# Fewer identity products, later small products and two-block tiles in the first pass of a graph kernel

## The chip, the cores and the metric

The kernel runs on one core of one Trainium2 chip. The metric is the device time in microseconds (us), the median of several runs. A profile of one execution goes with it; its span runs from the first to the last instruction and is about one microsecond shorter than the time. Engine names in the profile: PE is TensorE (products), PEld its weight loads, DVE is VectorE, ACT is ScalarE, POOL is GpSimd, SP is the engine that issues most loads.

## The reference, cut to what matters

Two graph layers on x (3327 nodes, 512 features) with one adjacency matrix (3327 x 3327, sparse in content, stored dense, all float32).

```python
h = relu(layernorm(x))
h1 = relu(adj @ (h @ W1) + b1)            # W1: 512 x 128
x = x + adj @ (h1 @ W2) + b2              # W2: 128 x 512
h = relu(layernorm(x))
# attention over the nonzero entries of adj, and a second aggregate adj @ h, both gated
e = where(adj != 0, exp(-leaky_relu(s_left[:, None] + s_right[None, :], 0.01)), 0)
x_a = (e / (sum(e) + 1e-5)) @ (h @ W_sa)
x_b = adj @ (h @ W_gcnb) + b_gcnb
x = x + sigmoid(attn_a * x_a + attn_b * x_b)
```

## The kernel before

The rows are padded to 26 blocks of 128, and the columns of the transposed adjacency are cut into six chunks of 512 and one of 256 (chunks 0 to 6). The kernel goes through the adjacency twice. The first pass makes adj @ (h @ W1) and at the same time finds, for every block of 32 columns, which rows hold a nonzero, so that the second layer can gather those rows alone. The second pass makes adj @ h1, then @ W2, and the second layer's features. A third part combines the gathered rows.

At its head, while the first blocks of x are loaded, TensorE multiplies an identity with itself:

```python
WAKE = 30
...
    awake = bank(psB, "awake")
    for _ in range(WAKE):
        nc.tensor.matmul(awake[:, :P], ident, ident, start=True, stop=True)
```

Loads of the adjacency go through a pool of eight buffers of 128 x 512. The helper can put n blocks into one buffer; the first pass asks for one block at a time, the second pass for as many as fit (two in the chunk of 256 columns):

```python
        def load_adj(j, c, name, n=1):
            c0, w = chunks[c]
            n = min(n, NB - j)
            t = adjp.tile([P, CW], F32, tag="adj", name=f"{name}_{c}_{j}")
            t = t[:, : n * w].rearrange("p (k i) -> p k i", i=w)
            rows = adjT[j * P : (j + n) * P, c0 : c0 + w]
            nc.sync.dma_start(t, rows.rearrange("(k p) i -> p k i", p=P))
            return t
```

The first pass, cut. Per block j and chunk c there is one big product into acc_u on TensorE and one row-maximum (`most`) on VectorE. In chunk 0 the blocks of x are normalized, transposed (pt), and multiplied by W1 (pu) on the way:

```python
        for c in range(NCH):
            c0, w = chunks[c]
            acc = bank(psA, f"acc_u_{c}")
            most = l0w.tile([P, MG, NB], F32, tag="most", name=f"most_{c}")
            for j in range(NB):
                if c == 0:
                    ...                       # load_x, normalize, turn_h (pt), make_u (pu)
                with queued(x_loaded[min(j + 4, NB - 1)] if c == 0 else None):
                    a = load_adj(j, c, "a1")[:, 0, :]
                added = nc.tensor.matmul(
                    acc[:, :w], u[j], a[:, :w], start=(j == 0), stop=(j == NB - 1)
                )
                with queued(scaled[min(j + 3, NB - 1)] if c == 0 else None):
                    nc.vector.tensor_reduce(
                        most[:, : w // GW, j], a[:, :w].rearrange("p (b i) -> p b i", i=GW),
                        axis=AX.X, op=ALU.max, apply_absolute_value=True,
                    )
                if j >= 2:
                    next(lists, None)         # one step of the previous chunk's lists
                if j % 3:
                    gather_behind(added)      # one gather of listed rows, on GpSimd
                ...
            chunk_end = make_g(c, acc)        # relu, transpose (pg), copies to g
            with tc.issue_after(chunk_end.ins):
                if c == 1:
                    load_weights()            # W2, the bias row b2 (b_row in the profile), W_sa, ...
                ...
            lists = make_lists(c, most)
            next(lists)
```

`load_weights` also has VectorE add 0.5 to the bias row, once it has landed. `make_lists` is a generator; each `yield` lets the loop above go one tile on. From the row-maxima it makes flags, a running count, offsets by two small products (p_off) and a shift by another (p_sh). Then, for one batch of column groups after another, VectorE makes comparisons (`at`), TensorE multiplies them with `step` in many small products (p_list), and VectorE turns the results into lists of rows (past, jb, row_h, row_a):

```python
            nc.vector.tensor_tensor(after[...], count[...], upto[...], ALU.subtract)
            p_off = bank(psB, f"p_off_{c}")
            nc.tensor.matmul(p_off[:, :n], before, count[:, :n], start=True, stop=True)
            nc.tensor.matmul(p_off[:, MG : MG + n], every, count[:, :n], start=True, stop=True)
            ...                                # offset, size, p_sh, step
            yield
            ...                                # column groups into batches of up to 18 rows of places
            for batch in batches:
                ...
                for i, q in batch:
                    r, k = rooms[i], col[i, q]
                    for h in range(2):
                        b = NQ * i + 2 * h + q - g0
                        nc.vector.tensor_scalar(                      # `at`
                            at[:, k : k + r, h, :],
                            place_row[:, : r * HALF].rearrange("p (k m) -> p k m", m=HALF),
                            offset[:, b : b + 1], None, op0=ALU.is_ge,
                        )
                    if (i, q) != batch[-1]:
                        yield
                pl = bank(psB, f"p_list_{f0}")
                for i, q in batch:
                    for k in range(col[i, q], col[i, q] + rooms[i]):
                        for h in range(2):
                            nc.tensor.matmul(                         # p_list
                                plv[h * HALF : (h + 1) * HALF, k, :], at[:, k, h, :],
                                step[:, NQ * i + 2 * h + q - g0, :], start=True, stop=True,
                            )
                yield
                ...                            # past, jb, row_h, row_a
                listed.update(batch)
                yield
```

A scheduler orders each engine's instructions after this program, so their places on an engine need not be those of the program text. After the first pass the vectors of weights for the scores are made: VectorE forms products of W_sa with a row (junk) and TensorE turns the columns (pw).

Of the kernel before, what the change touches and what calls it, by code (L numbers as in the profile page):

```python
# [19 lines left out]
CW = 512  # L20
# [4 lines left out]
LEAD = 3, 4  # L25
EH = 8
SEG = 4
WAKE = 30
LN_EPS = 1e-5
SUM_EPS = 1e-5  # L30
SLOPE = 0.01
# [15 lines left out]
def kernel(  # L47
# [20 lines left out]
    NB = NP // P  # L68
# [14 lines left out]
    def bank(pool, name):  # L83
        return pool.tile([P, CW], F32, tag="bank", name=name)
# [94 lines left out]
    def queued(*insts):  # L179

        behind = ExitStack()
        for inst in insts:
            if inst is not None:
                behind.enter_context(tc.issue_after(inst.ins))
        return behind
# [30 lines left out]
    with (  # L216
# [48 lines left out]
        x_loaded, scaled, h_turned, u_made = {}, {}, {}, {}  # L265
# [118 lines left out]
        def make_lists(c, most):  # L384


            c0, w = chunks[c]
            g0, n = c0 // GW, w // GW

            def small(shape, name, dtype, bufs=2):  # L390
                return l0w.tile(shape, dtype, tag=name, name=f"{name}_{c}", bufs=bufs)

            flag = small([P, MG, NB], "flag", BF16)
            nc.vector.tensor_scalar(flag[:, :n, :], most[:, :n, :], 0.0, None, op0=ALU.is_gt)

            upto = small([P, MG, NB], "upto", BF16)
            flat = "p b j -> p (b j)"
            nc.vector.tensor_tensor_scan(
                upto[:, :n, :].rearrange(flat), begin[:, :n, :].rearrange(flat),
                flag[:, :n, :].rearrange(flat), 0.0, op0=ALU.mult, op1=ALU.add,  # L400
            )
            count = small([P, MG], "count", BF16)
            nc.vector.tensor_copy(count[:, :n], upto[:, :n, NB - 1])
            after = small([P, MG, NB], "after", BF16)
            nc.vector.tensor_tensor(
                after[:, :n, :], count[:, :n].unsqueeze(2).to_broadcast([P, n, NB]),
                upto[:, :n, :], ALU.subtract,
            )
            p_off = bank(psB, f"p_off_{c}")
            nc.tensor.matmul(p_off[:, :n], before, count[:, :n], start=True, stop=True)  # L410
            nc.tensor.matmul(p_off[:, MG : MG + n], every, count[:, :n], start=True, stop=True)
            offset = small([P, MG], "offset", F32)
            nc.vector.tensor_copy(offset[:, :n], p_off[:, :n])
            nc.vector.tensor_tensor(
                size[:, g0 : g0 + n], p_off[:, MG : MG + n], limit[:, g0 : g0 + n], ALU.is_gt
            )


            step = steps[c % 2]
            p_sh = bank(psB, f"p_sh_{c}")  # L420
            nc.tensor.matmul(
                p_sh[:, : n * NB], shift, after[:, :n, :].rearrange(flat), start=True, stop=True
            )
            nc.vector.tensor_tensor(
                step[:, :n, :NB], p_sh[:, : n * NB].rearrange("p (b j) -> p b j", j=NB),
                upto[:, :n, :], ALU.add,
            )
            yield
            batches = []
            for i in range(c0 // P, (c0 + w) // P):  # L430
                for q in range(2 if rooms[i] else 0):
                    if not batches or sum(rooms[k] for k, _ in batches[-1]) + rooms[i] > CW // NT:
                        batches.append([])
                    batches[-1].append((i, q))
            for batch in batches:
                col = {}
                m = 0
                for i, q in batch:
                    col[i, q] = m
                    m += rooms[i]  # L440
                f0 = first[batch[0][0]] + batch[0][1] * rooms[batch[0][0]]
                at = l0w.tile([P, CW // NT, 2, HALF], BF16, tag="at", name=f"at_{f0}")
# [4 lines that stand above are left out]
                        nc.vector.tensor_scalar(  # L447
                            at[:, k : k + r, h, :],
                            place_row[:, : r * HALF].rearrange("p (k m) -> p k m", m=HALF),
                            offset[:, b : b + 1], None, op0=ALU.is_ge,  # L450
                        )
                    if (i, q) != batch[-1]:
                        yield
                pl = bank(psB, f"p_list_{f0}")
                plv = pl[:, : m * NT].rearrange("p (c j) -> p c j", j=NT)
                for i, q in batch:
                    for k in range(col[i, q], col[i, q] + rooms[i]):
                        for h in range(2):
                            nc.tensor.matmul(  # L459
# [4 lines that stand above are left out]
                past = l0w.tile([P, CW // NT, NB], BF16, tag="past", name=f"past_{f0}", bufs=1)  # L464
                nc.vector.tensor_tensor(
                    past[:, :m, :], plv[:, :, :NB],
                    place_col[:, f0 : f0 + m].unsqueeze(2).to_broadcast([P, m, NB]), ALU.is_le,
                )
                jb = l0w.tile([P, CW // NT], F32, tag="jb", name=f"jb_{f0}")
                nc.vector.tensor_reduce(jb[:, :m], past[:, :m, :], axis=AX.X, op=ALU.add)  # L470
                nc.vector.scalar_tensor_tensor(
                    jb[:, :m], jb[:, :m], float(P), plv[:, :, NB], op0=ALU.mult, op1=ALU.add
                )

                nc.vector.tensor_scalar(
                    row_h[:, f0 : f0 + m], jb[:, :m], float(NP - 1), None, op0=ALU.min
                )
                nc.vector.scalar_tensor_tensor(
                    row_a[:, f0 : f0 + m], jb[:, :m], float(NG), group_col[:, f0 : f0 + m],
                    op0=ALU.mult, op1=ALU.add,  # L480
                )
                listed.update(batch)
                yield
# [11 lines left out]
        for c in range(NCH):  # L495
            c0, w = chunks[c]
            acc = bank(psA, f"acc_u_{c}")
            most = l0w.tile([P, MG, NB], F32, tag="most", name=f"most_{c}")
            for j in range(NB):
                if c == 0:  # L500
                    if j + 4 < NB:
                        load_x(j + 4)
                    if j + 3 < NB:
                        normalize(j + 3)
                    if j + 2 < NB:
                        turn_h(j + 2)
                    if j + 1 < NB:
                        make_u(j + 1)
                with queued(x_loaded[min(j + 4, NB - 1)] if c == 0 else None):
                    a = load_adj(j, c, "a1")[:, 0, :]  # L510
                added = nc.tensor.matmul(  # L511
                    acc[:, :w], u[j], a[:, :w], start=(j == 0), stop=(j == NB - 1)
                )
# [6 lines that stand above are left out]
                    next(lists, None)  # L520
                if j % 3:
                    gather_behind(added)
                if c == 0 and j % 2 == 0:
                    with queued(scaled[min(j + 3, NB - 1)]):
                        next(constants, None)
            for work in (lists, constants):
                for _ in work:
                    pass
            chunk_end = make_g(c, acc)
            with tc.issue_after(chunk_end.ins):  # L530
                if c == 1:
                    load_weights()
                if 0 < c <= HUB_LOADS:
                    load_hub(c - 1)
            lists = make_lists(c, most)
            next(lists)

# [120 lines left out]
        for c in range(NCH):  # L658
            c0, w = chunks[c]
            acc = bank(psA, f"acc_g_{c}")  # L660
            per = CW // w
# [435 lines left out]
```

## Time and profile before

| | |
|---|---|
| time, median of 3 runs | 781.73 us (780.81 to 782.48) |
| span of the profile | 780.7 us |
| first pass, chunk 0 from its first big product | 13.50 to 67.36 us |
| first pass, chunks 1 to 6 | 67.36 to 224.86 us |
| second pass and the rest | 224.86 to 780.7 us |
| TensorE busy over the span | 755.4 us (97%) |
| VectorE busy over the span | 517.5 us (66%) |
| big products acc_u | 364 records, 580 ns each |
| row-maxima `most` | 182, 640 ns each |
| small products p_list | 456 records of 128 x 27, 186 ns each |

Each float32 product shows as two records, and records of neighbouring products overlap, so a record's length is not what it costs; the distance from start to start is. A line of a timeline has start, duration, engine, source line, operation, output and inputs, shapes and how many instructions it merges; square brackets name the idle time before it and what ended it. A line of waits has engine, what waited, for whom, then the total in us, how many times, and the longest.

### The profile page before, as it was taken

To read this page: it belongs to the slowest core of one execution; us is meant where nothing else is said; L and a number is where in the kernel's file an instruction comes from. 1 tells how busy PE (TensorE), PEld (TensorE's weight loads), DVE (VectorE), ACT (ScalarE), POOL (GpSimd) and SP (SyncE) were. 2 spreads that over 40 slices of the span, in tenths; PEclk is the share of its full clock that TensorE was granted. 3 is DMA by queue.
4 is the path that set the end of the run, shared out by engine and by line. 5 is a ranking of instruction groups with operands and counts; after the bars stand their busy time and mean duration, and the time that the engine had idled before them with its cause. 6 is when DMAs were issued, how large, how long until landed. Compare 5 with 4: busy or idle time off the path is not lost.

```text
span 780.7 us, 12235 instructions
## 1 busy us (share of the span) xinstructions
PE 755.4 (97%) x3647; PEld 415.5 (53%) x3647; DVE 517.5 (66%) x1658; ACT 185.5 (24%) x396; POOL 489.8 (63%) x513
## 2 busy tenths in 40 slices
PE   9999989999999999999999999999999999999995
PEld 8775434444544344344446456665665666655453
DVE  6768979999992876759577575555465464644542
ACT  6882000000000331403215212221221221311211
POOL 1400746666777777777773277677777777777720
PEclk9999999999999999999999999999999999999998
DMA  7888899889889999899998578688888888888840
GB/s 241 247 261 262 272 296 289 263 270 293 230 262 288 319 333 336 283 323 318 311 336 266 171 226 242 202 245 255 252 238 253 251 234 260 225 258 229 228 154 32
DMA packets 107099, 200.15 MB, mean 256 GB/s; under 512 B 17009, under 2 KB 30864, under 8 KB 107024
## 3 DMA queue, kind: packets, MB, share of 16 engines
q1 hardware_dynamic: 72800, 124.40, 48.7%
q0 software_dynamic: 25536, 63.74, 29.8%
q10 hardware_dynamic: 8688, 11.15, 4.3%
q8 instruction: 31, 0.51, 0.3%
q14 instruction: 44, 0.36, 0.2%
HBM read 179.39 MB, written 20.55 MB: 256 GB/s over the span
## 4 chain that ended last, share of the span: by engine, by line
PE 82%; DMA 7%; DVE 7%; issue 1%; ACT 1%; POOL 0%; SPq 0%; POOLq 0%; ACTq 0%; DVEq 0%
PE acc_u L511 16%; PE acc_g L665 14%; PE acc L809 13%; PE p_b L863 12%; PE p_a L870 11%; DMA a<-in_adjT_dram 6%; PE ptt L823 3%; PE pu L293 3%; PE acc_hub L624 2%; PE px L580 2%; PE p_list L459 2%; PE pt L285 1%; DVE junk L559 1%; DVE xb L583 1%; PE awake L100 1%
## 5 line engine op out<-in xcount | busy, mean ns | idle before, releaser
L139 POOL DMA_INDIRECT ae<-in_adjT_dram,row_a x228 | 244.2, 1071 | 145.2 <-DVE most L515 49.1
L139 POOL DMA_INDIRECT hr<-h_rows,row_h x140 | 143.5, 1025 | 47.0 <-issue 27.4
L511 PE MATMUL acc_u<-a,rows 128*128 128x512 f32 (+1 forms) x364 | 164.0, 580 | 1.5 <-DMA a<-in_adjT_dram 1.5
L665 PE MATMUL acc_g<-a,g 128*128 128x512 f32 (+1 forms) x364 | 156.4, 570 | 3.6 <-DMA a<-in_adjT_dram 3.4
L139 POOL DMA_INDIRECT rows<-h_rows,row_h x88 | 90.0, 1022 | 50.7 <-DVE e_hub L206 24.2
L515 DVE TENSOR_REDUCE most<-a 128x16 f32<-128x512 f32 (+1 forms) x182 | 111.1, 640 | 7.2 <-DMA a<-in_adjT_dram 6.8
L665 PEld LDWEIGHTS acc_g<-a,g 128*128 128x128 f32 x364 | 68.2, 192 | 80.1 <-issue 62.7
L863 PE MATMUL p_b<-W_g_sb,tyT 128*128 128x257 f32 x416 | 97.1, 386 | 0.8 <-ACT tyT L836 0.5
L870 PE MATMUL p_a<-W_sa_sb,tyT 128*128 128x512 f32 (+2 forms) x216 | 93.5, 577 | 0.0
L863 PEld LDWEIGHTS p_b<-W_g_sb,tyT 128*128 128x128 f32 x416 | 76.6, 189 | 30.8 <-DVE ae L206 7.3
L511 PEld LDWEIGHTS acc_u<-a,rows 128*128 128x128 f32 x364 | 63.9, 192 | 52.3 <-issue 45.8
L838 DVE COPY tyT<-ptt 128x512 f32<-128x512 f32 x51 | 34.9, 686 | 73.6 <-PE ptt L823 73.5
L809 PE MATMUL acc<-hr,ae 64*64 64x512 f32 x560 | 68.0, 607 | 0.0
L870 PEld LDWEIGHTS p_a<-W_sa_sb,tyT 128*128 128x128 f32 x216 | 41.0, 190 | 37.7 <-issue 35.9
L728 ACT ACTIVATE f<-f 128x2 f32<-128x2 f32 x26 | 5.3, 203 | 173.2 <-DVE f L727 145.8
L809 PE MATMUL acc<-rows,ae 64*64 64x512 f32 x352 | 42.5, 594 | 2.5 <-issue 1.8
L809 PEld LDWEIGHTS acc<-hr,ae 64*64 64x64 f32 x560 | 29.8, 136 | 23.4 <-issue 22.9
L302 ACT ACTIVATE gT<-acc_u,b_col 128x512 f32<-128x512 f32 (+1 forms) x7 | 4.6, 656 | 154.8 <-PE acc_u L511 97.9
L696 DVE TENSOR_TENSOR xb<-xb,b_row 128x512 f32<-128x512 f32 x26 | 17.7, 690 | 29.7 <-DMA xb<-in_x_dram 24.1
L559 DVE SCALAR_TENSOR_TENSOR junk<-rows,w_rows 128x512 bf16<-128x512 f32 x52 | 35.7, 687 | 1.9 <-ACT rows L201 0.9
L583 DVE TENSOR_TENSOR xb<-px,xb 128x512 f32<-128x512 f32 x26 | 16.9, 683 | 24.9 <-PE px L580 24.9
L823 PEld LDWEIGHTS ptt<-ident,ty 128*128 128x128 f32 x208 | 24.2, 141 | 14.2 <-issue 12.9
(142 smaller groups left out, 909.9 us busy)
## 6 DMA issues: line engine op xcount, KB each, us to landing
a<-in_adjT_dram SPq DMA_DIRECT2D x325, 256.0 KB, 4.0
h_rows<-rows SPq DMA_DIRECT2D x26, 260.0 KB, 4.1
x<-in_x_dram SPq DMA_DIRECT2D x26, 256.0 KB, 3.4
xb<-in_x_dram SPq DMA_DIRECT2D x26, 256.0 KB, 5.0
x<-xb ACTq DMA_DIRECT2D x26, 256.0 KB, 2.1
x1b<-x SPq DMA_DIRECT2D x26, 256.0 KB, 4.9
out_dram<-va SPq DMA_DIRECT2D x25, 256.0 KB
ae<-in_adjT_dram,row_a POOLq DMA_INDIRECT x228, 4.4
```

The costliest lines, as they stand in the source:

```text
L139: return nc.gpsimd.indirect_dma_start(out=dst, out_offset=None, in_=table, in_offset=bass.IndirectOffsetOnAxis(ap=rows, axis=0), bounds_ch ...
L293: nc.tensor.matmul(pu[:, :HID], hT[:, k, :], W1_sb[:, k, :], start=(k == 0), stop=(k == KD - 1))
L511: added = nc.tensor.matmul(acc[:, :w], u[j], a[:, :w], start=(j == 0), stop=(j == NB - 1))
L515: nc.vector.tensor_reduce(most[:, : w // GW, j], a[:, :w].rearrange("p (b i) -> p b i", i=GW), axis=AX.X, op=ALU.max, apply_absolute_value ...
L559: return nc.vector.scalar_tensor_tensor(junk, h, 1.0, w_rows[:, s, :], op0=ALU.mult, op1=ALU.mult, accum_out=into)
L583: nc.vector.tensor_tensor(x1, px, x1, ALU.add)
L665: added = nc.tensor.matmul(acc[:, :w], g[j], a[:, j % per, :], start=(j == 0), stop=(j == NB - 1))
L809: added = nc.tensor.matmul(taken[i]["acc"][h][q * HALF : (q + 1) * HALF, :], both[half_p, q * n + k, :], taken[i][k0][k][half_p, q, :D], s ...
L823: moved = nc.tensor.transpose(pt[:, k * P : (k + 1) * P], ty[h][:, k * P : (k + 1) * P], ident)
L838: last = nc.vector.tensor_copy(dst, src)
L863: nc.tensor.matmul(p_b[n][:, :WH], tyT[:, k, 0, :], W_g_sb[:, k, n * WH : (n + 1) * WH], start=(k == 0), stop=(k == KD - 1),)
L870: last = nc.tensor.matmul(p_a[:, c0:c1], tyT[:, k, 1, :], W_sa_sb[:, k, c0:c1], start=(k == 0), stop=(k == KD - 1),)
```

## The change

The change has three parts, all in the first pass. The head has 18 identity products instead of 30, to let TensorE go on to the first real work sooner. The generator of the lists yields once more before the products p_off, and after the last comparison of each batch too, so that a tile of other work lies between comparisons and the products that read them. And in the chunk of 256 columns, two blocks share one buffer and one load, as the second pass already has it. No arithmetic is added or removed but the twelve identity products.

```diff
-WAKE = 30
+WAKE = 18
@@ make_lists
                 upto[:, :n, :], ALU.subtract,
             )
+            yield
             p_off = bank(psB, f"p_off_{c}")
@@ make_lists, in each batch
                             offset[:, b : b + 1], None, op0=ALU.is_ge,
                         )
-                    if (i, q) != batch[-1]:
-                        yield
+                    yield
                 pl = bank(psB, f"p_list_{f0}")
@@ first pass
             acc = bank(psA, f"acc_u_{c}")
+            per = CW // w
             most = l0w.tile([P, MG, NB], F32, tag="most", name=f"most_{c}")
@@ first pass, for each j
-                with queued(x_loaded[min(j + 4, NB - 1)] if c == 0 else None):
-                    a = load_adj(j, c, "a1")[:, 0, :]
+                if j % per == 0:
+                    with queued(x_loaded[min(j + 4, NB - 1)] if c == 0 else None):
+                        tile_a = load_adj(j, c, "a1", per)
+                a = tile_a[:, j % per, :]
```

## The prediction

> **What bounds the kernel now.** I read the page first, then the windows of the first pass cut at each chunk's first product, then the waits of TensorE there, then the timeline of the two stretches that looked odd. The change touches only the first pass (0 to 225 us of the 780.7 us span), so only that pass is worked out.
>
> The windows give one row for each of chunks 2 to 6 (columns: length, busy time and instructions of each engine, granted clock, DMA share, GB/s):
>
> ```profile
> 93.84:126.31 32.47, 28.89 (x149) 12.88 (x147) 26.75 (x69) 0.69 (x1) 17.79 (x19) 0.95 0.91 293
> 126.31:154.28 27.97, 27.62 (x136) 11.64 (x135) 27.04 (x70) 0.69 (x1) 17.26 (x18) 1.00 0.88 269
> 154.28:180.07 25.79, 25.79 (x125) 11.40 (x124) 24.68 (x64) 0.69 (x1) 17.02 (x18) 1.00 0.91 281
> 180.07:205.89 25.82, 25.82 (x121) 11.29 (x119) 24.56 (x64) 0.69 (x1) 17.04 (x18) 1.00 0.89 270
> 205.89:224.86 18.97, 17.44 (x108) 10.50 (x107) 17.63 (x65) 0.69 (x1) 14.32 (x15) 1.00 0.74 207
> ```
>
> The reader should see two engines close together: TensorE (first busy column) is never idle in chunks 4 and 5, but VectorE (third) is busy for all but 1.1 to 1.3 us of them, and chunk 3 has 27.04 us of VectorE work in 27.97 us. Chunk 2 stands out with 32.47 us and a clock of 0.95. Chunk 6 has a low DMA share, 0.74. The waits of TensorE from 68 to 225 us:
>
> ```profile
> PE p_list L459 <- DVE at L447: 2.8, 2, 2.5
> PE acc_u L511 <- DMA a<-in_adjT_dram: 1.5, 5, 0.4
> PE p_sh L421 <- DVE after L405: 0.9, 1, 0.9
> PE p_off L410 <- DVE count L403: 0.2, 1, 0.2
> ```
>
> Only 5.4 us of real waiting, most of it in chunk 2. Its timeline shows why:
>
> ```profile
> 99.14 0.31 DVE L447 TENSOR_SCALAR at<-place_row,offset 128x384 bf16<-128x384 f16 x1
> 102.39 0.43 DVE L257 TENSOR_SCALAR b_row<-b_row 128x512 f32<-128x512 f32 x1 [2.94 <-DMA b_row<-in_b_dram]
> 102.73 1.23 DVE L447 TENSOR_SCALAR at<-place_row,offset 128x384 bf16<-128x384 f16 x5
> ...
> 100.35 0.20 PE L459 MATMUL p_list<-step,at 128*64 128x27 bf16 x1
> 103.10 1.42 PE L459 MATMUL p_list<-step,at 128*64 128x27 bf16 x35 [2.54 <-DVE at L447]
> ```
>
> The bias row's load lands late, VectorE stands behind it for 2.94 us, the comparisons `at` come late, and TensorE stands at the small product. The granted clock is then 0.78 from 101 to 106 us and 0.84 from 106 to 110. The head:
>
> ```profile
> 1.43 8.59 PE L100 MATMUL awake<-ident 128*128 128x128 f32 x60 [1.43 <-POOL ident masks.py:199]
> 6.22 1.50 ACT L201 ACTIVATE h<-x,ln_a 128x512 f32<-128x512 f32 x2
> 9.86 1.04 PE L285 MATMUL pt<-ident,h 128*128 128x128 f32 x8
> ```
>
> The first normalized block is made from 6.22 to about 7.0 us, but its transposes begin only at 9.86, after the identity products.
>
> **What the Trainium skill says.** TensorE: Matmul & The Clock Gate, Part 1 (the HAM clock gate): TensorE starts at half rate and is released after a busy window of about 3.4 us, and an idle window throttles it again. The trace agrees: the identity products' records stand 213 ns apart up to 4.86 us, 3.43 us after the first, and 112 ns apart from then on; after the 2.5 us stall of chunk 2 the granted clock is 0.5 from 103.9 to 107.2 us, so here less than a whole idle window was enough. The same page, Part 2, step-by-step, says that only TensorE pulls weight loads ahead while its products stay in order; its Part 1 calls VectorE's queue a strict FIFO. The trace agrees: the `at` that follow the late bias sit behind it. Perfetto Trace Analysis, Identifying the Most-Contended Engine, warns that a busy TensorE is no measure of its limit, while VectorE's occupancy is; hence I use start-to-start times for TensorE.
>
> **The change part by part.**
>
> *Identity products, 30 to 18.* Each is two records, so 24 records go. All that go run at the fast rate: 24 x 0.112 = 2.68 us. The last would then end near 7.2 us, and the first block is ready near 7.0, so TensorE hardly waits. What follows is the transposes, ScalarE's copy (0.64 us after their start, so 7.8 us; ScalarE is free at 7.91 instead of copying at 10.50) and the rest of the pipeline. Chunk 0 then runs at a period of 2.19 us a tile with TensorE continuous. The loads can follow: the windows show 366 GB/s at 6 to 8 us and only 127 GB/s at 12 to 14, so there was a lull to use. I take the 10.50 - 7.91 = **2.6 us**.
>
> *More work between comparisons and small products.* The order of the two built programs shows what the scheduler makes of it. Before, it cut the small products of a batch into pieces between the big ones: in the loops of chunks 1 to 6 there are 4, 6, 9, 5, 5 and 9 runs of p_list. In the changed program there are 3, 3, 4, 2, 2 and 6, so 38 become 20, with the same products in all. What does a run cost? In chunk 4, a big product takes 0.857 us start to start among its like, and 1.05 us when it stands alone after a run (160.96 to 162.01): 0.19 more. The run itself is 0.24 us for 8 (162.01 to 162.25) and 0.49 for 24 (160.47 to 160.96), so 0.0156 a product and 0.115 fixed. The fixed part is 0.19 + 0.115 = 0.30 us a run, and 18 fewer are **5.4 us of TensorE time**. The p_off pair moves behind two big products and so loses its waits of 0.2 us, and p_sh its 0.9 us.
>
> But the 5.4 us can't all be had, because VectorE's work is unchanged (2574 instructions in both). Chunk by chunk:
> - Chunk 1: a run fewer and 0.2 us of wait: 0.5 us.
> - Chunk 2: the late bias stays. It landed 8.55 us after the chunk's first product (93.84 to 102.39) and is loaded at the same point. In the changed order all six `at` of the first batch stand behind it, so the run of 36 begins near 8.55 + 0.43 + 0.31 = 9.3 us and ends near 10.4, almost as before (10.6). But seven big products lie ahead of it instead of five: 2 x 0.86 = 1.7 us gained, and after it come 2 runs instead of 5: 0.9 us. A full-rate clock would give up to 1.5 more. That makes 28.3 to 29.8 us of 32.5.
> - Chunks 2 to 6 by VectorE: from the bias on, 20.4 us of work in chunk 2 (what is busy from there on, less one row-maximum that now comes earlier, plus one `at`), then 27.0, 24.7, 24.6 and 17.6 from the windows: 114.3 us. It also waited some 0.5 us a chunk for p_list, 2.5 in all. Starting at 8.98 us after the chunk's first product this ends at 126 us, against 131.0 for the five windows. TensorE by itself would need about 120. So VectorE takes over as the bound there and the gain is **5 us**, up to 6.5 where it may finish behind TensorE.
>
> *Half chunk's tiles of two blocks.* Chunk 6 asks for 13 tiles of 256 KB instead of 26 of 128 KB; eight buffers now hold 16 blocks. Its last nine products took 218.60 to 224.86 = 6.26 us, while nine at the undisturbed 0.44 us need 4.0. The five waits for loads (1.5 us) should go. VectorE, whose row-maxima ran up to 3.5 us behind in this chunk, then sets its end, so this is inside the 5 us above and not added. The pass-two tiles are asked for earlier, which may save part of the second pass's 3.4 us of load waits.
>
> *Against it.* In the second pass's first chunk the transposes pw now stand in eight places instead of two runs: 6 x 0.2 = 1.2 us more, part of it hidden behind loads (DMA share 0.96 from 225 to 235 us). I take 0.6.
>
> Sum: 2.6 + 0.5 + 5.4 - 0.6 = 7.9 us (5.4 lies between 5 and 6.5). From 781.7 us this gives **about 773.5 us**.
>
> **The rivals.**
> 1. *The second pass swallows it:* its DMA share is 0.94 to 1.05. If its loads set its length and an earlier start gave no earlier loads, half would be lost, 777 to 778 us. Against: the loads of a tile follow the release of its buffer by a product, so they move along with it, and the first pass has DMA to spare (0.74 to 0.91).
> 2. *VectorE is not the bound:* it ran ahead of TensorE at the end of every chunk but the last (row-maximum 1.4 to 2 us before its product). If it can catch up in more places, the 5.4 us of runs and all waits come home: 769 to 770 us.
> 3. *The batched products turn into waits:* a run of 32 needs all eight comparisons, and `past` the whole run. If VectorE falls behind, TensorE stands at each run, and a stop like chunk 2's costs 1.5 us of clock as well; the gain shrinks to the head's 2.6 us: 778 to 779 us. For it: VectorE has about 1 us of slack a chunk. Against: two more big products lie ahead of each run.
> 4. *The clock:* the granted clock is 0.5 in three stretches of about 3.4 us, from 104, 268 and 732 us on, each worth up to 1.7 us; they may come or go.
>
> **Range and chances.** The head's 2.6 us is the surest; the other terms run from 1.5 to 8 us. So 770 to 777.5 us. A gain over 2% would need under 766.1 us, more than all TensorE terms give; a loss of 2% needs a new stall of 15 us, of which I see none. Faster 0.02, same 0.96, slower 0.02.
>
> **What would show it.** Right: the first pt near 7.2 us, the first product of the second pass near 217 us, chunk 2 at 28 to 30 us, p_list without waits in chunks 3 to 5, no load waits in chunk 6, lengths of chunks 3 to 5 near VectorE's busy time. Wrong: the first products of chunk 0 waiting for x, waits of p_list for `at` in several chunks, a second pass longer than the 556 us it has.

## The result and the profile after

| | before | changed |
|---|---|---|
| time, median of 6 runs each | 782.71 us | 770.02 us (768.03 to 772.05) |
| ratio | 1 | 0.9836, 95% interval 0.9813 to 0.9859 |
| span of the profile | 780.7 us | 766.1 us |
| chunk 0's first big product | 13.50 us | 12.02 us |
| chunk 1 | 26.48 us | 25.55 us |
| chunks 2 to 6 together | 131.02 us | 120.9 us |
| second pass and the rest | 555.84 us | 553.77 us |

The change gained 12.7 us by the medians, where I had expected 8.2. The two profiles differ by 14.6 us, because the one after is of the fastest of its six executions (768.03 us, which is 1.9 us more than its span). The windows of the changed kernel, cut at the first products of chunks 2 to 6 and of the second pass (columns as before: length, then busy time and instructions of PE, PEld, DVE, ACT and POOL, clock, DMA share, GB/s):

```profile
91.43:121.45 30.02, 27.31 (x148) 12.02 (x147) 26.57 (x70) 0.69 (x1) 17.74 (x18) 1.00 0.98 318
121.45:147.67 26.22, 26.10 (x136) 11.79 (x135) 26.03 (x69) 0.69 (x1) 17.06 (x18) 1.00 0.91 282
147.67:172.56 24.89, 24.89 (x125) 11.32 (x124) 24.71 (x64) 0.69 (x1) 17.09 (x18) 1.00 0.93 295
172.56:197.38 24.82, 24.82 (x121) 11.26 (x120) 24.64 (x65) 0.69 (x1) 17.24 (x18) 1.00 0.94 297
197.38:212.33 14.95, 14.86 (x108) 11.18 (x107) 14.12 (x56) 0.69 (x1) 11.60 (x12) 1.00 0.84 241
212.33:766.10 553.77, 534.88 (x2438) 291.27 (x2436) 327.17 (x1123) 134.68 (x284) 386.58 (x366) 1.00 0.82 254
```

Every chunk from 1 on is shorter, chunk 6 most: 14.95 us instead of 18.97. Chunk 2 is still far longer than its neighbours. The waits of TensorE from 60 us to the second pass:

```profile
PE p_list L459 <- DVE at L448: 2.2, 2, 1.9
PE acc_u L514 <- DMA a<-in_adjT_dram: 0.3, 1, 0.3
```

The waits for p_off and p_sh and nearly all waits for loads are gone; one wait of 1.9 us for the comparisons is left, in chunk 2. VectorE's timeline and TensorE's at that place:

```profile
99.55 0.43 DVE L257 TENSOR_SCALAR b_row<-b_row 128x512 f32<-128x512 f32 x1 [2.63 <-DMA b_row<-in_b_dram]
99.90 1.23 DVE L448 TENSOR_SCALAR at<-place_row,offset 128x384 bf16<-128x384 f16 x5
...
100.27 1.51 PE L459 MATMUL p_list<-step,at 128*64 128x27 bf16 x36 [1.86 <-DVE at L448]
```

As worked out beforehand, VectorE still stands behind the late bias row, for 2.63 us, and all 36 small products follow in one run. The head:

```profile
1.43 7.11 PE L100 MATMUL awake<-ident 128*128 128x128 f32 x36 [1.43 <-POOL ident masks.py:199]
8.38 1.04 PE L285 MATMUL pt<-ident,h 128*128 128x128 f32 x8
```

The transposes begin at 8.38 us, not at 7.2: in this execution the identity products' records stood 213 ns apart up to 7.4 us, while in the execution of before it was up to 4.86 us. The profile before also has a stretch of half clock in chunk 2 (mean clock 0.95), and this one has none there.

### The profile page after: what moved, and what is told of

It reads as the page before. It is cut to its first block, busy times and chain, and to the rows that moved or that the text cites. A ratio compares the mean times of both kernels' runs of the same rounds, so it can differ in the third digit from the quotient of the medians.

```text
span 766.1 us, 12162 instructions
## 1 busy us (share of the span) xinstructions
PE 742.6 (97%) x3623; PEld 411.1 (54%) x3623; DVE 515.5 (67%) x1658; ACT 185.6 (24%) x396; POOL 490.7 (64%) x513
## 4 chain that ended last, share of the span: by engine, by line
PE 77%; DVE 12%; DMA 6%; issue 2%; ACT 1%; POOL 1%; SPq 0%; POOLq 0%; ACTq 0%; DVEq 0%
PE acc_g L668 14%; PE acc L812 13%; PE p_b L866 12%; PE acc_u L514 12%; PE p_a L873 12%; DMA a<-in_adjT_dram 4%; DVE most L518 4%; PE pu L293 3%; PE ptt L826 3%; PE acc_hub L627 2%; PE px L583 2%; DVE junk L562 2%; PE pt L285 1%; DVE at L448 1%; DMA xb<-in_x_dram 1%
## 5 line engine op out<-in xcount | busy, mean ns | idle before, releaser
L514 PE MATMUL acc_u<-a,rows 128*128 128x512 f32 (+1 forms) x364 | 157.6, 569 | 0.4 <-DMA a<-in_adjT_dram 0.3
L812 PE MATMUL acc<-hr,ae 64*64 64x512 f32 x560 | 66.2, 593 | 0.0
L586 DVE TENSOR_TENSOR xb<-px,xb 128x512 f32<-128x512 f32 x26 | 16.9, 682 | 21.8 <-PE px L583 21.8
```

Source lines behind the costliest of these rows:

```text
L514: added = nc.tensor.matmul(acc[:, :w], u[j], a[:, :w], start=(j == 0), stop=(j == NB - 1))
L812: added = nc.tensor.matmul(taken[i]["acc"][h][q * HALF : (q + 1) * HALF, :], both[half_p, q * n + k, :], taken[i][k0][k][half_p, q, :D], s ...
```

## The experiments

Each ratio is to the kernel before, run alternately on the same chip in five rounds. Medians of different chips differ (784 to 786 us for the kernel before on four of them), so ratios are compared, not times. In us, one per mille is about 0.8.

The theory after the result (A): the parts add up, and TensorE sets the pace of the first pass: runs of small products, its waits, the loads of chunk 6 and the head. Its rivals: VectorE's amount of work bounds chunks 2 to 6 (the prediction's step), the second pass swallows what the first gains, or only the removed waits count and not the runs.

**One part alone: the head.**

```diff
-WAKE = 30
+WAKE = 18
```

> The kernel before with 18 identity products instead of 30 and nothing else. Theory A (head shift): chunk 0 begins its first big product 1.5 to 2.7 us earlier, depending on when the full clock is granted in that run, the rest moves along with it: 1.5 to 2.7 us off the time, ratio 0.9965 to 0.998. Rival B (the loads or the second pass swallow it): first big product earlier, but the second pass begins at the same time or lasts longer by as much: ratio 0.999 to 1.001.

Measured: 0.9989 (0.997 to 1.0009). The profile has the first big product at 11.96 us, 1.54 earlier. The interval holds both a gain of 2.4 us and none, so this run alone doesn't decide whether the shift reaches the end.

**One part alone: the two yields.**

```diff
+            yield
             p_off = bank(psB, f"p_off_{c}")
...
-                    if (i, q) != batch[-1]:
-                        yield
+                    yield
```

> The kernel before with the two later yields alone (30 identity products, one block a tile in chunk 6). Theory A (TensorE time of runs and waits comes home): chunks 1 to 5 shorter by about 0.9, 2.5, 1.7, 0.9 and 1.0 us as in the changed kernel, chunk 6 by up to 1 us, so 6 to 8 us, ratio 0.990 to 0.992. Rival B (VectorE is the bound, as the prediction had it): chunks 2 to 6 together gain 5 us or less, with chunk 6 about as long as before: ratio 0.993 to 0.994.

Measured: 0.9889 (0.986 to 0.9918), some 8.7 us, the largest part. The windows of its chunks 3, 4, 5 and 6:

```profile
123.71:149.82 26.11, 26.03 (x136) 11.79 (x135) 25.92 (x69) 0.69 (x1) 16.95 (x18) 1.00 0.91 283
149.82:174.70 24.88, 24.88 (x124) 11.32 (x123) 24.85 (x64) 0.69 (x1) 17.10 (x18) 1.00 0.93 297
174.70:199.52 24.82, 24.82 (x120) 11.26 (x119) 24.61 (x65) 0.69 (x1) 17.22 (x18) 1.00 0.90 278
199.52:218.78 19.26, 16.67 (x108) 10.32 (x106) 17.18 (x65) 1.16 (x2) 14.69 (x16) 1.00 0.73 200
```

Chunks 3 to 5 have the changed kernel's lengths within 0.1 us. Chunk 6 keeps its length, and TensorE waits in it for loads:

```profile
PE acc_u L511 <- DMA a<-in_adjT_dram: 2.0, 5, 0.7
```

So chunk 6 belongs to the third part: theory A had given it up to 1 us here, and the rival was right that it stays. In chunks 4 and 5 TensorE is never idle, in the kernel before as well as here, so their lengths show what a run costs: five runs each before (25.79 and 25.82 us) and two each now (24.88 and 24.82) make 0.30 and 0.33 us a run. The point estimate of the whole is past theory A's 6 to 8 us, but its interval (6.4 to 11.0 us) reaches into that range and stays clear of rival B's 5 us.

**One part alone: two blocks a tile in chunk 6.**

```diff
+            per = CW // w
...
-                with queued(x_loaded[min(j + 4, NB - 1)] if c == 0 else None):
-                    a = load_adj(j, c, "a1")[:, 0, :]
+                if j % per == 0:
+                    with queued(x_loaded[min(j + 4, NB - 1)] if c == 0 else None):
+                        tile_a = load_adj(j, c, "a1", per)
+                a = tile_a[:, j % per, :]
```

> The kernel before with two blocks a tile in chunk 6 alone. Theory A (the loads bound the end of chunk 6): chunk 6 of 18.97 us falls to 15 to 16.5 us, no waits for loads in it: 2.5 to 4 us, ratio 0.995 to 0.997. Rival B (VectorE bounds chunk 6, the prediction's step): chunk 6 falls by 1 us or less, its busy VectorE time being 17.6 us: ratio about 0.999.

Measured: 0.9954 (0.9934 to 0.9974), some 3.6 us. Chunk 6:

```profile
205.91:222.43 16.52, 15.88 (x108) 11.36 (x107) 15.49 (x58) 0.69 (x1) 12.20 (x13) 1.00 0.80 224
```

It falls from 18.97 to 16.52 us and none of its products waits for a load. That is theory A's forecast. One doubt: in this order the scheduler also moved two of VectorE's products for the scores' weights (0.69 us each) out of chunk 6.

**VectorE's products held out of chunk 6, with one block a tile.**

```diff
-                nc.vector.scalar_tensor_tensor(
-                    junk, W_sa_sb[:, k, :], 1.0, a_row, op0=ALU.mult, op1=ALU.mult,
-                    accum_out=col[:, k : k + 1],
-                )
+                with queued(seen):            # the first pass's last row-maximum
+                    nc.vector.scalar_tensor_tensor(
+                        junk, W_sa_sb[:, k, :], 1.0, a_row, op0=ALU.mult, op1=ALU.mult,
+                        accum_out=col[:, k : k + 1],
+                    )
```

> The kernel before, one block a tile in chunk 6, but VectorE's products of the weights for the scores are held behind the last row-maximum of the first pass; two of them, 0.69 us each, stood inside chunk 6. Theory A (loads bound the end of chunk 6): chunk 6 shortens by 0.5 us or less, ratio 0.9995 to 1.001. Rival B (what shortened chunk 6 is that VectorE's work left it): chunk 6 shortens by 1.4 us or more, ratio 0.998 or less.

Measured: 0.9983 (0.9953 to 1.0013). The interval holds both expectations: inconclusive. The only profile is of the longest execution (792.2 us), but its chunk 6 ran at full clock. There those products all stand behind the last row-maximum, chunk 6 still takes 20.31 us, and TensorE waits in it 1.6 us for loads, in four waits. So nothing there shows that VectorE's products were what lengthened chunk 6; one profile doesn't rule out that they bring a part of the 3.6 us.

**The whole change again, and with 30 identity products.**

```diff
-WAKE = 18
+WAKE = 30
```

> The changed kernel again, beside the next three on one chip. Both theories: ratio 0.982 to 0.986; first big product near 12.0 us if the full clock is granted late (7.4 us), near 10.9 us if it is granted at 4.9 us.

> The changed kernel with 30 identity products again. Theory A (24 records at the head cost 2.6 us at the same moment of the full clock, and the shift reaches the end): 2 to 2.7 us slower than the changed kernel, ratio to the kernel before 0.986 to 0.988. Rival B (the head's shift is swallowed later): as the changed kernel within 0.5 us.

Measured on one chip: 0.9842 (0.9809 to 0.9875) and 0.9865 (0.9827 to 0.9904). The difference, 1.8 us, points to theory A, but the intervals overlap. What the profiles show of the head is sharper, because the moment at which the identity products become fast differs between executions:

| run | identity products | fast from | first big product |
|---|---|---|---|
| before | 30 | 4.86 us | 13.50 us |
| with 30 again | 30 | 4.88 us | 13.50 us |
| yield before p_off alone | 30 | 7.54 us | 14.77 us |
| changed kernel | 18 | 7.38 us | 12.02 us |
| changed kernel, third time | 18 | 5.51 us | 11.12 us |
| the two yields alone | 30 | 5.88 us | 13.97 us |
| changed kernel, bias addition later (below) | 18 | 5.79 us | 11.26 us |
| half row-maxima | 18 | 4.36 us | 10.98 us |

At nearly the same moment (5.88 and 5.79, or 7.54 and 7.38) twelve products are worth 2.7 us, and 2.5 between moments half a microsecond apart (4.86 and 4.36); a late moment costs up to 1.3 us more. In every one of these runs chunk 0 then lasts 53.86 us, so the head's shift is passed on whole to chunk 1. That it reaches the end of the kernel is likely from there on, and not shown by the times.

**The yield after each batch's last comparison alone, and the yield before p_off alone.**

```diff
# the first
-                    if (i, q) != batch[-1]:
-                        yield
+                    yield
# the second
+            yield
             p_off = bank(psB, f"p_off_{c}")
```

> The kernel before with the yield after the last comparison of each batch alone. p_list then has 3, 3, 3, 3, 2 and 7 or so runs in chunks 1 to 6 instead of 4, 6, 9, 5, 5 and 9. Theory A (each run costs TensorE 0.30 us): 16 fewer runs are 4.8 us, and waits for comparisons in chunk 2 shrink; p_off and p_sh wait as before: ratio 0.992 to 0.995. Rival C (it is the waits of p_off and p_sh that the change removes, not the runs): ratio 0.998 or more.

> The kernel before with the yield before p_off alone. p_list has 5, 6, 6, 5, 4 and 9 runs in chunks 1 to 6. Theory A: 3 fewer runs are 0.9 us and the waits of p_off and p_sh go, 1.1 us: 2 us, ratio 0.997 to 0.998. Rival C (the waits are what counts): 4 us or more, ratio under 0.995.

Measured: 0.9923 (0.9893 to 0.9953), 6.0 us, with 3, 3, 4, 3, 2 and 7 runs; and 0.9974 (0.9955 to 0.9992), 2.0 us. Both fall where theory A put them, by the number of runs, and neither where rival C did, though the first interval alone (3.7 to 8.4 us) would allow other prices of a run. Together they make the 8.7 us of the two yields, within the intervals. The changed kernel's timeline shows the price of a run once more:

```profile
155.59 0.68 PE L459 MATMUL p_list<-step,at 128*64 128x27 bf16 x32
156.19 5.42 PE L514 MATMUL acc_u<-a,rows 128*128 128x512 f32 x12
161.54 0.68 PE L459 MATMUL p_list<-step,at 128*64 128x27 bf16 x32
```

A run of 32 takes 0.60 us (155.59 to 156.19), where 0.115 + 32 x 0.0156 = 0.61 had been worked out. The six big products behind it take 5.35 us instead of 6 x 0.857 = 5.14: again 0.2 us for coming after a run.

**The bias addition one chunk later, in the changed kernel and in the one before.**

```diff
# in load_weights, after chunk 1
-            nc.vector.tensor_scalar(b2_row, b2_row, 0.5, None, op0=ALU.add)
# at the end of chunk 2
+                if c == 2:
+                    nc.vector.tensor_scalar(b2_row, b2_row, 0.5, None, op0=ALU.add)
```

> The changed kernel with the addition of 0.5 to the bias row one chunk later in the program, so that it stands on VectorE behind the last row-maximum of chunk 2 and its load has long landed. Nothing is left out. Theory A (that stop of 2.6 us on VectorE is what remains of chunk 2's excess, and it takes the clock down in some runs): chunk 2 falls from 30.0 to 25.5 to 27 us, p_list has no wait in it, and the clock is not halved near 105 us: 3 to 5 us under the changed kernel, ratio to the kernel before 0.978 to 0.981. Rival B (VectorE's amount of work bounds chunk 2): chunk 2 stays over 28.5 us, ratio 0.982 or more.

> The same displacement of the addition in the kernel before. Theory A: the stop of 2.9 us and the half clock after it leave chunk 2, the runs of p_list stay (5 in chunk 2, as many as before elsewhere): 3 to 5 us, chunk 2 from 32.5 to 28 us, ratio 0.994 to 0.996. Rival B: 1.5 us or less, ratio 0.998 or more.

Measured: 0.9826 (0.9791 to 0.9862) and 0.9958 (0.994 to 0.9977). In the kernel before it gains 3.3 us, as theory A said, but chunk 2 takes 29.67 us and not 28. In the changed kernel it gains hardly more than 1 us, which isn't clear of the noise, and chunk 2 still takes 29.46 us: theory A fell there, and rival B's figures came. But rival B's reason isn't what the trace shows: VectorE is busy for only 5.06 of the 8 us from 98 to 106. TensorE's timeline of the changed kernel with the displaced addition shows the new wait:

```profile
97.57 0.74 PE L457 MATMUL p_list<-step,at 128*64 128x27 bf16 x36
98.24 2.03 PE L512 MATMUL acc_u<-a,rows 128*128 128x512 f32 x4
102.11 1.12 PE L512 MATMUL acc_u<-a,rows 128*128 128x512 f32 x2 [1.83 <-DMA a<-in_adjT_dram]
103.65 1.13 PE L512 MATMUL acc_u<-a,rows 128*128 128x512 f32 x2 [0.42 <-DMA a<-in_adjT_dram]
105.55 1.13 PE L512 MATMUL acc_u<-a,rows 128*128 128x512 f32 x2 [0.78 <-DMA a<-in_adjT_dram]
```

p_list comes at once, and then the products wait for tiles. The changed kernel's loads issued from 91.4 to 104 us say why (output and input, queue, how many, KB each, and for the first the us to landing):

```profile
a<-in_adjT_dram SPq DMA_DIRECT2D x8, 256.0 KB, 9.7
W_sa_sb<-in_W_sa_dram ACTq DMA_DIRECT2D x1, 1024.0 KB
w_own<-in_w_self_dram ACTq DMA_DIRECT2D x1, 512.0 KB
W_sb<-in_W_dram ACTq DMA_DIRECT2D x1, 256.0 KB
b_row<-in_b_dram ACTq DMA_DIRECT2D x1, 256.0 KB
```

Two MB of weights are loaded at once at the end of chunk 1, and a tile then lands after 9.7 us, where over the whole span the median is 4.0. The late bias row (256 KB) is loaded in the same burst; that the burst is what delays it was not tested apart from the tiles.

**Row-maxima over half of each group, in the changed kernel.** It leaves out half of the search in chunks 1 to 6, so that its lists miss rows.

```diff
-                        most[:, : w // GW, j], a[:, :w].rearrange("p (b i) -> p b i", i=GW),
+                        most[:, : w // GW, j],
+                        a[:, :w].rearrange("p (b i) -> p b i", i=GW)[:, :, : GW // 2 if c else GW],
```

> The changed kernel, but the row-maxima of chunks 1 to 6 read only the first half of each group of 32 columns: it leaves out half of the search, so its lists of rows miss some. VectorE has some 8 us less work in each of chunks 1 to 5; p_list has 3, 3, 3, 2, 2 and 2 runs. Theory A (VectorE does not bound chunks 3 to 5 of the changed kernel): they keep 25.7 to 26.2, 24.6 to 24.9 and 24.6 to 24.8 us; only chunk 6 may fall, by 1 to 2 us through its four fewer runs. Rival B (VectorE bounds them): chunks 3 to 5 fall by 1 us or more each.

Its windows of chunks 3 to 6:

```profile
121.64:147.27 25.63, 25.55 (x137) 11.68 (x135) 23.19 (x78) 0.69 (x1) 18.12 (x18) 1.00 0.92 288
147.27:172.06 24.79, 24.79 (x124) 11.33 (x123) 19.04 (x65) 0.69 (x1) 16.97 (x18) 1.00 0.94 295
172.06:196.80 24.74, 24.74 (x121) 11.28 (x120) 18.73 (x64) 0.69 (x1) 17.00 (x18) 1.00 0.94 291
196.80:211.73 14.93, 14.86 (x108) 11.91 (x107) 13.71 (x62) 0.69 (x1) 11.40 (x12) 1.00 0.91 270
```

VectorE is busy for 19.04 us of chunk 4 instead of 24.71, and the chunk takes 24.79 us instead of 24.89. Chunk 3 gives 0.6 us; its one run fewer explains 0.3 of that. VectorE's amount of work does not bound the changed kernel's chunks 4 and 5. (Chunk 2 isn't compared: products for the scores' weights moved into it, and its mean clock is 0.89.) In chunk 6 I was wrong: two runs instead of six should have saved 1.2 us, and nothing came, because the first is now paced by its comparisons and takes 2.2 us instead of the 0.67 that 36 products cost:

```profile
202.06 2.23 PE L459 MATMUL p_list<-step,at 128*64 128x27 bf16 x36
```

A run merged further than its comparisons are ready gives its saving back as a slow run. The ratio of the whole, 0.9858 (0.9827 to 0.9889), is not under the changed kernel's either.

**The weights' loads spread over chunks 1 to 5, with the displaced addition.** Nothing is left out.

```diff
# in load_weights, after chunk 1: W2 and the bias row stay
-            nc.scalar.dma_start(W_sa_sb, W_sa.rearrange("(k p) f -> p k f", p=P))
-            nc.scalar.dma_start(w_own, w_self.partition_broadcast(P))
-            nc.scalar.dma_start(bab_row, b_ab.partition_broadcast(P))
# at the chunks' ends
+                if c in (2, 3, 4, 5):
+                    k = c - 2
+                    nc.scalar.dma_start(W_sa_sb[:, k, :], W_sa[k * P : (k + 1) * P, :])
+                if c == 3:
+                    nc.scalar.dma_start(w_own, w_self.partition_broadcast(P))
+                    nc.scalar.dma_start(bab_row, b_ab.partition_broadcast(P))
```

> The changed kernel with the addition to the bias row one chunk later, and the weights' loads spread: at the end of chunk 1 only W2 and the bias row are loaded, W_sa in four parts at the ends of chunks 2 to 5, the gates' rows at the end of chunk 3. Nothing is left out. Theory A (the burst of 2 MB of weights at the start of chunk 2 takes the bandwidth from the tiles, whose landing then takes 8.9 us, and was the wait behind the one for the bias): chunk 2 falls from 29.5 us to 25.5 to 26.5 us, its products wait for no load, other chunks stay within 0.5 us; 3 to 4 us under the version with the addition displaced alone, ratio to the kernel before 0.977 to 0.980. Rival B (the loads are short on bandwidth in every chunk, so the burst only moves): chunks 3 to 5 lengthen by what chunk 2 gains, ratio 0.982 to 0.984.

Measured: 0.9964 (0.9945 to 0.9983), on a chip where the kernel before itself took 854.66 us and TensorE's products p_b stood for 21.8 us with no wait that the profile shows. This can't be set beside the other ratios, so it was run again on another chip with its two neighbours:

> The changed kernel with the bias addition one chunk later and the weights' loads spread over the ends of chunks 1 to 5, on one chip with the next two. Theory A (the burst of 2 MB of weights delays the tiles of chunk 2): chunk 2 falls to 25.5 to 26.5 us without waits for loads, 3 to 4 us under the version with the addition displaced alone. Rival B (the burst only moves): chunks 3 to 5 lengthen by what chunk 2 gains, and the time is that of the version with the addition displaced, within 1 us.

> The changed kernel with the bias addition displaced alone. Both theories: chunk 2 of 29 to 30 us with waits for tiles, 1 us or so under the changed kernel.

> The changed kernel: ratio to the kernel before 0.982 to 0.986, chunk 2 of 30 to 30.5 us with a wait of p_list for comparisons of about 2 us.

Measured: spread loads 0.9812 (0.9784 to 0.984), 769.58 us; displaced addition alone 0.9836 (0.9802 to 0.987), 771.65 us; changed kernel 0.9861 (0.9822 to 0.9899), 772.31 us. Chunk 2 of the displaced addition, in this profile and in the first one of the same kernel, and chunks 2 to 4 with spread loads:

```profile
91.05:121.26 30.21, 27.86 (x149) 11.90 (x148) 26.72 (x70) 0.69 (x1) 18.05 (x19) 0.94 0.97 316
90.66:120.12 29.46, 26.43 (x148) 11.47 (x147) 26.01 (x69) 0.69 (x1) 18.05 (x18) 1.00 0.98 322
```

```profile
91.36:118.88 27.52, 26.64 (x148) 11.82 (x147) 26.13 (x69) 0.69 (x1) 18.22 (x19) 1.00 0.93 286
118.88:145.50 26.62, 26.20 (x137) 11.90 (x135) 26.43 (x70) 0.69 (x1) 17.25 (x18) 1.00 0.91 290
145.50:170.80 25.30, 25.21 (x124) 11.14 (x123) 24.92 (x65) 0.69 (x1) 17.17 (x18) 1.00 0.98 317
```

Chunk 2 loses 2.7 us against the first of these, which had a stretch of half clock in it (0.94), and 1.9 us against the second, which like the spread version had the full clock. TensorE waits in it only 0.45 us for a load, where it had waited 2.3 and 3.0 us. Chunk 4 gets 0.4 us longer than in both profiles of the displaced addition (24.88 us); chunk 3 had 26.00 us in the one and 26.63 in the other, so its 26.62 say nothing. Chunks 2 to 6 together take 119.66 us instead of 120.87 and 120.86. So theory A holds for the waits, but of what chunk 2 gains only 1.2 us are left at the pass's end, part of it having moved as rival B said; and chunk 2 stays 1 us over what A had promised, for which no cause is shown. By its medians this version is 2.7 us ahead of the changed kernel on the same chip, but the intervals of the two overlap, so that it is faster is likely and not shown.

## Why the prediction was right and wrong

- **The head, 2.6 us: mechanism right.** At the same moment of the clock it is 2.7 us. All 24 records that go stand behind the change of rate, early or late, so the 112 ns I had priced them at holds. The two profiles show 1.48 us, because the changed kernel's was taken with the late moment (7.38 against 4.86 us). I had taken that moment for fixed: the 3.43 us after the first product that I read from one profile lie between 2.9 and 6.1 us in the executions of the table. That my one profile fitted so well was luck.
- **The runs, 0.30 us each and 5.4 us in all: right.** Chunks 4 and 5 give 0.30 and 0.33 us a run, the run of 32 has the length that was worked out, and the two yields apart gained 6.0 and 2.0 us. The second pass kept the gain, against the first rival: it begins at 212.33, 213.42 and 212.41 us in three profiles of the changed kernel instead of 224.86, 11.4 to 12.5 us earlier, and the times of the three measurements fall by 11.6 to 12.7 us.
- **"VectorE takes over as the bound there and the gain is 5 us": the step that failed.** Chunks 2 to 6 gained 10.1 us, to 120.9 us (121.4 and 121.9 in the repeats, with half clock in chunk 2 as before), next to the 120 I had put down for TensorE alone, not the 126 for VectorE. The run with half row-maxima shows who sets the pace: with 5.7 us less work for VectorE in chunk 4 and 5.9 in chunk 5 they keep their lengths within 0.1 us. For chunks 2, 3 and 6 no run shows it so cleanly. What was wrong in my sum is seen in VectorE's stretch from the end of the bias addition to its last row-maximum in the changed kernel:

```profile
99.98:213.67 113.69, 112.35 (x615) 55.34 (x616) 111.49 (x309) 3.22 (x5) 75.77 (x75) 1.00 0.93 292
```

  I had put down 114.3 us of work and 2.5 us of waits; it was 111.5 and 2.2. Of the work too many, 1.8 us are products for the scores' weights (junk_w), which the scheduler had placed in chunk 6 before (two of them are shown), and which stand behind the pass in the changed kernel; and 0.4 us are the scan for the next list, begun before chunk 4 and counted in chunk 3's window:

```profile
153.88 1.01 DVE L398 TENSOR_TENSOR_SCAN upto<-begin,flag 128x416 bf16<-128x416 bf16 x1
222.57 0.68 DVE L546 SCALAR_TENSOR_TENSOR junk_w<-W_sa_sb,a_row 128x512 bf16<-128x512 f32 x1
224.59 0.68 DVE L546 SCALAR_TENSOR_TENSOR junk_w<-W_sa_sb,a_row 128x512 bf16<-128x512 f32 x1
```

  The bias row came 0.4 us earlier after the chunk's start. And I let the pass end with VectorE, while in the changed kernel the second pass begins 1.3 us before VectorE is through. The 2.8 and 0.3 us of VectorE's time, these 0.4 and these 1.3 make the 5 us between 126 and 120.9. VectorE was not far from a bound all the same: it is busy for 98% of this stretch. A further saving of TensorE's time alone may meet it; no run tests that.
- **"This is inside the 5 us above and not added" (two-block tiles): failed with it.** Alone the tiles gain 3.6 us, and chunk 6 goes from 18.97 us to 16.52 with them and to 14.95 with all parts. Its waits for loads went with them; that the loads alone set its length isn't shown, as said above. The parts alone gain 0.9, 8.7 and 3.6 us, 13.2 together, so they add up within the intervals. The second rival, 769 to 770 us with VectorE not the bound, came nearest.
- **Chunk 2 at 28.3 to 29.8 us: too short.** I had 28.3 for a full clock, and it took 30.02 with it; with half clock, for which I had 29.8, it took 30.44 and 30.52. The wait for the bias came where I put it. I had not seen that the tiles are late there too.
- **The second pass, 0.6 us lost to pw: not seen.** It came out 2.07 us shorter in this pair, but its length differs by more among executions of the changed kernel (553.77, 556.78 and 558.11 us), so neither is shown.
- **Slips that changed little.** 781.7 - 7.9 is 773.8, not 773.5. From 218.60 us on the timeline has eight products of chunk 6, not nine. The second pass's DMA share goes down to 0.90 in the windows that I used, not to 0.94.

## What to carry to other kernels

Busy time of a window says how much work fell into it, not how much belongs to it: work for a later part may fill an engine's free time there, and an engine that runs ahead carries work across the cut. A near-full engine is shown to be a bound only when less of its work makes the stretch shorter. Count how often a stream of large products is interrupted by small ones, not only how many small ones there are: each interruption cost 0.30 us here, and two more yields, which let the operands be ready first, merged 38 runs into 20. After a wait is removed, look at what else the same burst of loads delays before counting the gain.

## What was not expected of the hardware

The identity products became fast at moments between 4.36 and 7.54 us in different executions, and with this the first big product moved: with 30 of them it began between 13.32 us (two-block tiles alone) and 14.77 us. In the changed kernel's repeats a stall of about 2.2 to 2.5 us in chunk 2 was followed by a stretch of half clock, as in the kernel before; in its first profile, with 1.86 us, it was not. The longest stall alone doesn't decide it: with the displaced addition, waits of 1.5 us at most were followed by half clock in one execution, and one of 1.83 us in another was not. And one of the five chips of the experiments ran the unchanged kernel 9% slower; in the profile of the variant taken there TensorE pauses for up to 9.7 us at a time without a visible wait.
